# Attention on one Trainium2 core: the product with the values in 64x32 tiles of the array, fed by an exchange of weight quarters

## The chip, the cores and the metric

The kernel runs on one core of a Trainium2 chip. A core has five engines with instruction lists of their own: TensorE (PE in the profile; its weight loads are listed apart as PEld), VectorE (DVE), ScalarE (ACT), GpSimd (POOL) and SyncE (SP), which here only issues transfers (DMA). The engines wait for each other by semaphores; each works through its list in order. The metric is the device time of one execution in microseconds; runs are compared by their median.

## The reference

Cross attention of 16 batches with 1024 queries of 512 features and 64 context rows, 16 heads of 32, all in float32.

```python
xq  = (1 + scale_q)  * layernorm(x)       + shift_q     # scale, shift: silu(cond) @ Wss + bss
xkv = (1 + scale_kv) * layernorm(context) + shift_kv
q = (xq @ Wq + bq).reshape(B, Lq, 16, 32)
k, v = split(xkv @ Wkv + bkv)
scores = einsum('bqhd,bkhd->bhqk', q, k) / sqrt(32)
attn = softmax(scores, axis=-1)
o = einsum('bhqk,bkhd->bqhd', attn, v).reshape(B, Lq, 512)
return x + (o @ Wp + bp)
```

## The kernel before

**Blocks.** The 16 x 1024 query rows are cut into 32 blocks of 512 rows (NB = 32, two to a batch, BPB = 2). The context of eight batches at a time forms a group, "A" and "B". All lists are written out by hand: the order of the calls in the program is the order on each engine (`tc.manual_schedule()`).

**Way in.** Up to block 2 the calls stand one by one: the context's keys and values, the first blocks' features and queries, and the first score products. Then follows the loop over i = 3 to 29, and a way out written by hand.

**One turn of the loop.** It works on several blocks at once: scores of block i, value product and projection of a = i - 1, the rest of the projection of b = i - 2, queries of n = i + 1, features of f = i + 2, normalising and turning of i + 3. The query product and the projection are each done as seven products of half size with sums made beforehand (`seven` at line 547, `product` at line 958). Their sums are made on GpSimd (`feature_sums`, line 506; `row_sums`, lines 928 to 938).

**Scores.** `score_products` (line 666) makes for each half z of the 64 keys 16 matmuls, 32 rows (features of a head) by 32 columns (keys) by 512 queries. The result lies with partition 32 c + key for the four head groups c, and the four heads r of a group side by side. `maximum` and `maxima` (lines 683, 703, 712) find the maximum of each row and spread it into the tile mb, whose buffer has the tag "spread" and exists once; `subtract` (line 725, GpSimd) and `weights` (line 731, ScalarE's exponential) follow. So the weights of a block are two tiles, `s_tiles[i, 0]` and `s_tiles[i, 1]`, one for each half of the keys.

**Sums of the weights.** `total` (line 765, GpSimd) adds the two tiles, `row_total` (line 770) sums over the keys, `inverse_rows` takes the reciprocal (line 785), writes it to memory (`ltd`, line 788) and reads it back in another order by four transfers (`vr`, line 790). `spread_rows` (line 796) spreads it into vb, and `divided` (lines 809 and 814) multiplies the value product with it on its way out of the accumulators.

**Value product.** `mix` (line 834) has 32 matmuls: for each half z, head group c and head r one with 32 rows (the keys of that half), 32 columns (features of the head) and 512 queries; the second half adds onto the first in the accumulator. `V_all` holds the values to match: partition 32 c + key of the half, and along the free dimension batch, z and features. `value_move` (line 639) brings them there from `stages` in transfers of 32 partitions.

**Features.** `turn` (line 375) transposes 32x32 squares of normalised x into `ht` (one buffer); `move` (line 397) exchanges the squares between partition groups by 16 transfers of 64 KB into `xt` (two buffers); `scale_features` (line 455, ScalarE) applies scale and shift there.

**SyncE's list in the loop.** The two stores of block b (line 984), the residual's load (`load_residual`, line 127), the load of x (`load_x`, line 109), then `inverse_rows(i)`: the write ltd, a wait until it has landed, four reads vr; then the 16 transfers of `move(i + 3)`.

Of the kernel before, what the change touches and what calls it, by code (L numbers as in the profile page):

```python
# [20 lines left out]
def cross_attention_block(  # L21
# [369 lines left out]
    def move(i, two=False):  # L391

        ht = ht_tiles.pop(i)
        xt = features_tile(i)
        for k in range(4):
            for g in range(4):
                (nc.gpsimd if two and g % 2 else nc.sync).dma_start(  # L397
                    xt[32 * k : 32 * k + 32, g],
                    ht[32 * g : 32 * g + 32, k].rearrange("p c t b -> p c (t b)"),
                )  # L400
# [233 lines left out]
    def value_move(i, m):  # L634
        for c in (2 * m, 2 * m + 1):
            for j in range(2):
                for z in range(2):
                    at = j * LKV + z * HK
                    nc.sync.dma_start(
                        V_all[i][32 * c : 32 * c + 32, j::2, z, :],  # L640
                        stages[i][at : at + HK, :, c * P : (c + 1) * P],
                    )
# [115 lines left out]

    sum_tiles, lt_tiles, vt_rows = {}, {}, {}
# [22 lines left out]
    def inverse_rows(i):  # L782
# [3 lines left out]
        v = small.tile([P, NC, NJ], F32, tag="vr", name=f"vr_{i}")  # L786
        d = dram.tile([NC, 32, HPC, NJ], F32, tag="lt", name=f"ltd_{i}")
        nc.sync.dma_start(d.rearrange("c a r j -> (c a) r j"), lt)
        for r in range(HPC):
# [28 lines left out]
    def mix(i, apart=True, ks=(None,) * NC):  # L818
# [273 lines left out]
    turned_products()  # L1092
    turned_scaled(3)
    load_x(1)
    q_stats("B", (1,))
    load_x(2)
    turned_scaled(2)
    context_out("A", "v", 7)
    context_product("A", "k", 5)
    column_sums("q", w_q_sb, w_q_sums, (0,))  # L1100
    column_sums("q", w_q_sb, w_q_sums, (1,))
    context_out("A", "v", 5)
    load_projection()
    q_stats("B", (3,))
    turned_scaled(0)
    context_product("A", "k", 4)
    context_out("A", "k", 4)
    q_scale("B")
    context_out("A", "k", 5)
    q_stats(1, (0,))  # L1110
    turned_scaled(1)
    hidden("B", (3,))
    context_product("A", "v", 3)
    hidden("B", (2,))
    context_product("A", "k", 3)
    hidden("B", (1,))
    turned_features("B", 1)
    turned_features("B", 3)
    q_stats(1, (1,))
    hidden("B", (0,))  # L1120
    feature_sums(0, nc.gpsimd, (0,))
    turned_features("B", 0)
    feature_sums(0, nc.gpsimd, (1,))
    turned_features("B", 2)
    column_sums("q", w_q_sb, w_q_sums, (2,))
    context_out("A", "k", 3)
    q_stats(1, (3,))
    query_product(0, 1)
    feature_sums(0, nc.gpsimd, (2,))
    modulated("B", 0, 0, nc.scalar)  # L1130
    q_stats(1, (2,))
    q_scale(1)
    query_seed(0)
    modulated("B", 1, 0, nc.vector)
    context_product("A", "v", 4)
    context_out("A", "v", 3)
    hidden(1, (0,))
    modulated("B", 0, 0, nc.vector)
    hidden(1, (1,))
    turn(1, (0,))  # L1140
    load_x(3)
    hidden(1, (2,))
    load_projection_bias()
    query_product(0, 2)
    turn(1, (1,))
    turn(1, (2,))
    hidden(1, (3,))
    column_sums("q", w_q_sb, w_q_sums, (3,))
    turn(1, (3,))
    q_stats(2, (0,))  # L1150
    feature_sums(0, nc.gpsimd, (3,))
    q_stats(2, (3,))
    context_out("A", "v", 4)
    move(1, two=True)
    query_out(0, 2)
    query_product(0, 6)
    query_out(0, 6)
    modulated("B", 0, 1, nc.scalar)
    modulated("B", 1, 1, nc.vector)
    modulated("B", 0, 1, nc.vector)  # L1160
    modulated("B", 1, 1, nc.scalar)
    context_product("B", "k", 1)
    query_product(0, 5)
    feature_sums("B", nc.gpsimd, (0,))
    context_out("B", "k", 1)
    query_product(0, 7)
    q_stats(2, (1,))
    modulated("B", 1, 0, nc.scalar)
# [271 lines left out]
    for i in range(3, NB - 2):  # L1440
# [68 lines left out]
        if i + 3 < NB:  # L1509
            move(i + 3)  # L1510
# [138 lines left out]
```

## Time and profile before

| what | us |
|---|---|
| median of 3 runs (lowest to highest) | 1020.19 (1019.91 to 1021.4) |
| the profiled execution, its own time | 1021.49 |
| its span | 1019.7 |
| TensorE busy in the span | 1007.1 |
| VectorE / GpSimd / ScalarE busy | 864.3 / 808.1 / 637.6 |
| value product of one block, 64 records | 2.28 |
| score product of one half, 32 records | 1.07 |
| granted TensorE clock, mean of the span | 0.999 |

Columns of a row of groups are: line, engine, operation, output <- inputs, sizes, count. In a row of the stretches stand the stretch, its length and, engine by engine, busy time with the number of records that touch it, at the end the granted clock, the transfer engines' busy share and GB/s. A record that reaches over an edge is counted in both stretches. A matmul of float32 has two weight loads and two matmul records. In the time-ordered views the first two columns are start and length in us. SPq is SyncE's sequencer: an issue's length is the time that the list is occupied, not the transfer's.

### The profile page before, as it was taken

To read this page: it belongs to the slowest core of one execution; us is meant where nothing else is said; L and a number is where in the kernel's file an instruction comes from. 1 tells how busy PE (TensorE), PEld (TensorE's weight loads), DVE (VectorE), ACT (ScalarE), POOL (GpSimd) and SP (SyncE) were. 2 spreads that over 40 slices of the span, in tenths; PEclk is the share of its full clock that TensorE was granted. 3 is DMA by queue.
4 is the path that set the end of the run, shared out by engine and by line. 5 is a ranking of instruction groups with operands and counts; after the bars stand their busy time and mean duration, and the time that the engine had idled before them with its cause. 6 is when DMAs were issued, how large, how long until landed. Compare 5 with 4: busy or idle time off the path is not lost.

```text
span 1019.7 us, 21289 instructions
## 1 busy us (share of the span) xinstructions
PE 1007.1 (99%) x8109; PEld 770.6 (76%) x8109; DVE 864.3 (85%) x1184; ACT 637.6 (63%) x1025; POOL 808.1 (79%) x518
## 2 busy tenths in 40 slices
PE   8999999999999999999999999999999999999997
PEld 7887777777777777777777777877777778777746
DVE  6787889898889888988898888889888888876785
ACT  3688666666667666666666666666666666565520
POOL 2659898888898888888987887898888888987781
PEclk9999999999999999999999999999999999999999
DMA  9574544444445544444454453444543444345122
GB/s 301 199 217 131 150 173 146 126 133 150 156 156 165 167 128 127 134 153 153 151 168 131 127 165 123 152 160 157 167 142 116 124 158 153 112 126 168 44 77 95
DMA packets 112117, 149.82 MB, mean 147 GB/s; under 512 B 34024, under 2 KB 45312, under 8 KB 112016
## 3 DMA queue, kind: packets, MB, share of 16 engines
q1 hardware_dynamic: 111760, 147.95, 45.6%
q8 instruction: 64, 1.05, 0.4%
q0 software_dynamic: 256, 0.52, 0.2%
q14 instruction: 37, 0.30, 0.1%
HBM read 79.21 MB, written 34.60 MB: 112 GB/s over the span
## 4 chain that ended last, share of the span: by engine, by line
PE 88%; DVE 3%; POOL 3%; DMA 2%; ACT 1%; SPq 1%; issue 1%; DVEq 0%; POOLq 0%; ACTq 0%
PE pp L958 35%; PE pq L547 35%; PE po L834 7%; PE ps L666 6%; POOL s L725 2%; PE pp L861 1%; PE pk_A L547 1%; PE pv_A L547 1%; PE pk_B L547 1%; SPq L397 1%; ACT s L731 1%; DVE m L683 1%; DMA wss_kv<-in_L_xcond_Wss_kv_dram 1%; DMA x<-in_x_dram 1%; DVE mb L712 0%
## 5 line engine op out<-in xcount | busy, mean ns | idle before, releaser
L725 POOL TENSOR_TENSOR s<-s,mb 128x2048 f32<-128x2048 f32 x64 | 290.3, 4561 | 128.1 <-DVE mb L712 128.1
L692 ACT COPY s<-ps 128x1024 f32<-128x1024 f32 x128 | 129.4, 1012 | 102.6 <-DVE m L683 59.4
L683 DVE TRANSPOSE_TENSOR_REDUCE m<-ps 128x32 f32<-128x1024 f32 x128 | 151.4, 1217 | 33.2 <-PE ps L666 33.1
L958 PE MATMUL pp<-w_p_sb,ot 128*128 128x256 f32 x736 | 169.4, 380 | 1.3 <-DVE ot L814 0.9
L982 DVE TENSOR_TENSOR r<-pp,r 128x512 f32<-128x512 f32 x210 | 136.6, 671 | 30.0 <-PE pp L958 24.9
L958 PEld LDWEIGHTS pp<-w_p_sb,ot 128*128 128x128 f32 x736 | 139.9, 190 | 21.8 <-issue 1.8
L586 ACT ACTIVATE qt<-pq,bias_t 128x256 f32<-128x256 f32 x256 | 105.6, 463 | 74.0 <-PE pq L547 74.0
L731 ACT ACTIVATE s<-s 128x2048 f32<-128x2048 f32 x64 | 122.4, 1912 | 46.3 <-POOL s L725 46.2
L765 POOL TENSOR_TENSOR sum<-s,s 128x2048 f32<-128x2048 f32 x31 | 140.7, 4540 | 4.4 <-ACT s L731 4.4
L958 PEld LDWEIGHTS pp<-WT,s 128*128 128x128 f32 x496 | 89.8, 190 | 56.7 <-issue 28.5
L547 PE MATMUL pq<-xt_sums,w_q_sums 128*128 128x256 f32 x512 | 123.6, 385 | 0.0
L958 PE MATMUL pp<-WT,s 128*128 128x256 f32 x496 | 123.0, 391 | 0.0
L547 PE MATMUL pq<-xt,w_q_sb 128*128 128x256 f32 x512 | 121.4, 380 | 0.0
L547 PEld LDWEIGHTS pq<-xt_sums,w_q_sums 128*128 128x128 f32 x512 | 95.3, 190 | 34.2 <-issue 22.6
L547 PE MATMUL pq<-xt,w_q_sums 128*128 128x256 f32 x512 | 121.1, 380 | 0.0
L958 PE MATMUL pp<-WT,ot 128*128 128x256 f32 x496 | 117.3, 380 | 0.0
L547 PEld LDWEIGHTS pq<-xt,w_q_sb 128*128 128x128 f32 x512 | 97.1, 190 | 16.1 <-issue 3.4
L547 PEld LDWEIGHTS pq<-xt,w_q_sums 128*128 128x128 f32 x512 | 97.4, 190 | 13.3 <-ACT qt L586 0.3
L958 PEld LDWEIGHTS pp<-WT,ot 128*128 128x128 f32 x496 | 94.3, 190 | 13.4 <-POOL WT L896 0.8
L344 ACT ACTIVATE x<-x,rstdq 128x512 f32<-128x512 f32 x128 | 97.0, 808 | 2.0 <-POOL rstdq L319 2.0
L455 ACT ACTIVATE xt<-xt,ss_q 128x512 f32<-128x512 f32 x124 | 94.3, 808 | 5.5 <-DMA xt<-ht 3.8
L301 DVE BATCH_NORM_STATS2 bs<-x 128x6 f32<-128x512 f32 x128 | 87.0, 680 | 0.3 <-DMA x<-in_x_dram 0.3
(176 smaller groups left out, 1488.8 us busy)
## 6 DMA issues: line engine op xcount, KB each, us to landing
x<-in_x_dram SPq DMA_DIRECT2D x32, 1024.0 KB, 5.4
r<-in_x_dram SPq DMA_DIRECT2D x32, 1024.0 KB, 5.1
xt<-ht SPq DMA_DIRECT2D x488, 64.0 KB, 2.0
out_dram<-r SPq DMA_DIRECT2D x60, 512.0 KB, 3.7
wss_q<-in_L_xcond_Wss_q_dram SPq DMA_DIRECT2D x4, 512.0 KB, 10.1
vr<-ltd SPq DMA_DIRECT2D x128, 8.0 KB, 1.6
out_dram<-r SPq DMA_DIRECT2D x7, 256.0 KB, 2.2
x_A<-in_ctx_dram SPq DMA_DIRECT2D x4, 256.0 KB, 3.0
```

The source lines that it names most:

```text
L301: nc.vector.bn_stats(bs, r)
L344: nc.scalar.activation(dst, src, AF.Identity, bias=rstd[:, 1, j : j + 1], scale=rstd[:, 0, j : j + 1])
L455: nc.scalar.activation(xt[:, :, c, :], xt[:, :, c, :], AF.Identity, scale=ss["q"][:, c, b : b + 1], bias=ss["q"][:, NC + c, b : b + 1],)
L547: nc.tensor.matmul(out_, lhsT=lhsT, rhs=rhs, start=new and m == 0 and c == 0, stop=c == HC - 1, skip_group_check=True,)
L586: nc.scalar.activation(dst, src, AF.Identity, bias=bq_t[:, o : o + 1])
L683: nc.vector.tensor_reduce(m_tiles[i][:, z, 2 * e : 2 * e + 2, :], s_banks[i, z][e].rearrange("p r (j a) -> p r j a", a=32), AX.X, ALU.max, ...
L692: nc.scalar.copy(s_tiles[i, z][:, 2 * e : 2 * e + 2, :], s_banks[i, z][e])
L725: eng.tensor_tensor(s_tiles[i, z], s_tiles[i, z], mb_tiles[i], ALU.subtract)
L731: nc.scalar.activation(p, p, AF.Exp, scale=SCALE)
L765: nc.gpsimd.tensor_tensor(t, s_tiles[i, 0], s_tiles[i, 1], ALU.add)
L958: nc.tensor.matmul(acc[k][:, t * HO : (t + 1) * HO], lhsT=rows[:, c, t * P : (t + 1) * P], rhs=cols[:, c, :], start=n == 2 and t == 0 and ...
L982: nc.vector.tensor_add(r, a, r)
```

## The change

**Value product in 64x32 tiles.** For blocks 2 to 29 (`paired`) a matmul takes all 64 keys of a head at once: 16 matmuls of 64 rows by 32 columns by 512 queries, without adding up in the accumulator. The head groups go in the order 0, 2, 1, 3, so that rows 0 to 63 and rows 64 to 127 take turns. Blocks 0, 1, 30 and 31 keep the 32 matmuls.

**Exchange.** For that the two weight tiles of a block are rearranged: in each half of the partitions the upper quarter of the first tile and the lower quarter of the second change places, by way of a third tile `t` with the tag "spread" (mb's buffer). Three steps, each two transfers of 32 partitions x 4 x 512 floats.

**Values.** `value_move` takes one head group c a call and lays the values in the new order, but for the batch of blocks 0 and 1 and that of blocks 30 and 31, which keep the old one; their part goes by transfers of its own, 6 a call instead of 4.

**Order.** `inverse_rows` is split into `inverse_out` (reciprocal and write) and the reads; in the loop the swaps and parts of `move` are set between them. `load_residual(i)` stands ahead of `biased(a, 2)`. The way in, from `turned_products()` to the loop, is in a new order.

```diff
+    def paired(i):
+        return BPB <= i < NB - BPB
+    def swap(i, step):
+        if not paired(i):
+            return
+        first, second = s_tiles[i, 0], s_tiles[i, 1]
+        if step == 0:
+            swaps[i] = rpool.tile([P, HPC, TB], F32, tag="spread", name=f"swap_{i}")
+        t = swaps[i]
+        for at in (0, 64):
+            low, high = slice(at, at + 32), slice(at + 32, at + 64)
+            if step == 0:
+                nc.sync.dma_start(t[high], second[low])
+            elif step == 1:
+                nc.sync.dma_start(second[low], first[high])
+            else:
+                nc.sync.dma_start(first[high], t[high])
...
     def mix(i, apart=True, ks=(None,) * NC):
...
+        if paired(i):
+            for c in (0, 2, 1, 3):
+                rows = slice(64 * (c // 2), 64 * (c // 2) + 64)
+                for r in range(HPC):
+                    nc.tensor.matmul(
+                        po[c][32 * r : 32 * r + 32, :],
+                        lhsT=vt[rows, c % 2, 32 * r : 32 * r + 32],
+                        rhs=s_tiles[i, c % 2][rows, r, :],
+                        start=True,
+                        stop=True,
+                    )
+            return
...
-    def value_move(i, m):
+    def value_move(i, c):
+        for j in range(2):
+            for z in range(2):
+                at = j * LKV + z * HK
+                src = stages[i][at : at + HK, :, c * P : (c + 1) * P]
+                p = 64 * (c // 2) + 32 * z
+                dst = V_all[i][p : p + 32, j::2, c % 2, :]
+                plain = {("A", 0): 0, ("B", 1): NT - 1}.get((i, j))
+                if plain is None:
+                    nc.sync.dma_start(dst, src)
+                    continue
+                rest = slice(1, NT) if plain == 0 else slice(0, NT - 1)
+                nc.sync.dma_start(dst[:, rest], src[:, rest])
+                nc.sync.dma_start(
+                    V_all[i][32 * c : 32 * c + 32, 2 * plain + j, z, :], src[:, plain]
+                )
```

In the way in, the place that the prediction speaks of (as it stands after; in the list before, `move(1, two=True)` came ahead of `query_out(0, 2)`, `value_move("A", 0)` after it, and `scale_features(1, (1,))`, the first of them, after `query_out(0, 3)`):

```python
    query_product(0, 4)
...
    value_move("A", 0)
    move(1, two=True)
...
    context_product("B", "k", 2)
...
    scale_features(1, (0,))
    turn(2, (0,))
    query_product(0, 3)
    query_added(0, 4)
...
    query_out(0, 3)
...
    score_products(0, 0)
```

In the loop:

```diff
         added(b, 4)
         added(b, 3)
+        load_residual(i)
         biased(a, 2)
-        load_residual(i)
         mix(a)
...
         row_sums(a, 1)
+        swap(i, 0)
         if i < NB - 3:
             turn(i + 3, range(NT))
         if i < NB - 5:
             load_x(i + 5)
...
         query_product(n, 3)
         query_out(n, 3)
+        swap(i, 1)
         feature_sums(f)
         product(a, 7)
+        if i + 3 < NB:
+            move(i + 3, (0,))
         row_total(i)
+        inverse_out(i)
+        swap(i, 2)
+        if i + 3 < NB:
+            move(i + 3, (1,))
         inverse_rows(i)
         if i + 3 < NB:
-            move(i + 3)
+            move(i + 3, (2, 3))
```

More of the change, by code (lines that the diff above doesn't have):

```diff
@@ L1426, in cross_attention_block @@
+    subtract(2, zs=(1,))
+    biased(1, 2)
+    divided(1)
+    turn(5, (2,))
+    query_out(3, 7)
+    turn(5, (3,))
+    weights(2, 0)
+    scale_features(4, (1,))
+    weights(2, 1)
+    row_sums(1, 0)
+    load_residual(2)
+    swap(2, 0)
+    query_product(3, 5)
+    query_added(3, 5)
+    q_stats(6, (1,))
+    load_x(7)
+    product(1, 1)
+    total(2)
+    scale_features(4, (2,))
+    swap(2, 1)
+    added(1, 1)
+    query_product(3, 4)
+    product(1, 2)
+    q_stats(6, (3,))
     added(1, 2)
```

551 lines of the change are left out of this document (269 added, 282 removed).

## The prediction

> **What bounds the kernel now.** First the page's busy times and its chain of waits:
>
> ```profile
> span 1019.7 us, 21289 instructions
> PE 1007.1 (99%) x8109; PEld 770.6 (76%) x8109; DVE 864.3 (85%) x1184; ACT 637.6 (63%) x1025; POOL 808.1 (79%) x518
> PE 88%; DVE 3%; POOL 3%; DMA 2%; ACT 1%; SPq 1%; issue 1%; DVEq 0%; POOLq 0%; ACTq 0%
> PE pp L958 35%; PE pq L547 35%; PE po L834 7%; PE ps L666 6%; POOL s L725 2%; PE pp L861 1%; PE pk_A L547 1%; PE pv_A L547 1%; PE pk_B L547 1%; SPq L397 1%; ACT s L731 1%; DVE m L683 1%; DMA wss_kv<-in_L_xcond_Wss_kv_dram 1%; DMA x<-in_x_dram 1%; DVE mb L712 0%
> ```
>
> TensorE is the bound; what another engine saves is worth nothing unless TensorE waits for it. Where does it wait? The busy times of stretches (columns: stretch, length, then busy time and count of each engine):
>
> ```profile
> 40.00:70.00 30.00, 30.00 (x174) 25.58 (x174) 23.17 (x56) 27.05 (x66) 19.00 (x30) 1.00 0.64 201
> 70.00:104.00 34.00, 33.27 (x236) 25.62 (x243) 25.94 (x36) 27.35 (x46) 25.91 (x20) 1.00 0.50 141
> 166.00:966.00 800.00, 798.59 (x6553) 611.81 (x6552) 693.96 (x905) 516.11 (x800) 664.78 (x399) 1.00 0.45 142
> ```
>
> In 800 us of the loop it is free for 1.4, and between 40 and 104, in the way in that is reordered, for 0.73. So an edit pays only by taking work off TensorE, and costs only where its inputs come late. One turn of the loop in the chain, in order of time (start, length):
>
> ```profile
> 503.72 1.07 PE ps L666 x32
> ...
> 516.62 2.28 PE po L834 x62
> ...
> 533.00 1.07 PE ps L666 x32
> ```
>
> A turn is 533.00 - 503.72 = 29.28 us, of which the product with the values (po) is 2.28 and each score product (ps) 1.07.
>
> **The product itself.** [...] A score product is 16 matmuls on the 16 tiles of 32x32, two steps; the value product is 32 on the same 16 tiles, four steps. How these steps lie, by counts of records that touch a stretch (PE, then weight loads):
>
> ```profile
> 516.50:517.00 0.50, 0.45 (x16) 0.23 (x32) 0.00 (x0) 1.00 0.45 111
> 517.00:517.43 0.43, 0.43 (x32) 0.10 (x1) 0.00 (x0) 1.00 0.23 62
> 517.43:517.60 0.17, 0.17 (x17) 0.10 (x1) 0.00 (x0) 1.00 1.04 252
> 517.60:518.05 0.45, 0.45 (x31) 0.37 (x30) 0.00 (x0) 1.00 0.20 50
> ```
>
> Sixteen tiles stream together; the next sixteen follow at 517.00, 0.45 later; at 517.43 one tile has its successor, after a stream of 0.43, but the other fifteen, and their 30 weight loads, come only from 517.60 on. That hold of about 0.19 falls where the second half of the keys (z = 1) begins.
>
> Afterwards a matmul takes 64 rows and 32 columns, so 16 matmuls on 8 tiles: two on each, two passes each, again four steps. The number of instructions halves; the streaming doesn't. No row shows 64x32 tiles. From above: hold and spread as now, 2.28. From below, by instructions alone, half of 2.28, 1.14; excluded, since each tile must stream four times 0.43 = 1.72. Nearest is a product that also reuses tiles and also is only 16 matmuls, in the preamble, on 128x32 tiles, four tiles with eight steps:
>
> ```profile
> 28.52 1.08 PE L263 MATMUL ss_q<-wss_q,early 128*32 128x128 f32 x32
> 28.75:28.86 0.11, 0.11 (x12) 0.11 (x8) 0.00 (x0) 0.00 (x0) 1.00 1.07 382
> 28.86:28.97 0.11, 0.11 (x12) 0.11 (x8) 0.00 (x0) 0.00 (x0) 1.00 1.01 363
> ```
>
> Every step of 0.11 (a quarter of 0.43, with a quarter of the columns) has the same counts: no hold when a tile takes its next weights. So I take the score product, 16 matmuls without hold at 1.07, and add two steps of 0.43, less 0.05 as eight tiles start in half the spread of sixteen (about 0.1): 1.07 + 0.86 - 0.05 = **1.88**, 0.40 less than 2.28. Blocks 2 to 29: 28 x 0.40 = **11.2 us**.
>
> **What must be there in time.** Per block six transfers of 32 partitions x 8 KB (256 KB) join SyncE's list; their forms are not in the trace. Nearest rows: issues and landings by size, SyncE's queue, and who waits there:
>
> ```profile
> xt<-ht SPq DMA_DIRECT2D x488, 64.0 KB, 2.0
> vr<-ltd SPq DMA_DIRECT2D x128, 8.0 KB, 1.6
> x_A<-in_ctx_dram SPq DMA_DIRECT2D x4, 256.0 KB, 3.0
> L639 SPq DMA_DIRECT2D V_A<-stage_A x16: 587/602/668, 61.8 to 87.2; - x16
> 47.63 1.15 SPq L200 DMA_DIRECT2D w_p_sb<-in_L_xcond_Wp_dram  x1
> 505.15 0.34 SPq L788 DMA_DIRECT2D ltd<-lt  x1
> 508.48 1.75 SPq L790 DMA_DIRECT2D vr<-ltd  x4
> 510.32 11.35 SPq L397 DMA_DIRECT2D xt<-ht  x16
> ```
>
> An issue costs between 0.34 and 1.15 us; I take 0.60, the row that also is 32 partitions wide. Landing 3.0. The readers, on the other engines:
>
> ```profile
> 497.66 4.53 POOL L765 TENSOR_TENSOR sum<-s,s 128x2048 f32<-128x2048 f32 x1
> 504.57 0.55 DVE L785 RECIPROCAL lt<-lt 128x64 f32<-128x64 f32 x1
> 512.75 2.31 DVE L712 STREAM_TRANSPOSE mb<-m 128x2048 f32<-128x2048 f32 x1
> 514.99 2.27 DVE L796 STREAM_TRANSPOSE vb<-vr 128x2048 f32<-128x2048 f32 x1
> 517.18 1.25 DVE L982 TENSOR_TENSOR r<-pp,r 128x512 f32<-128x512 f32 x2
> 518.86 2.36 DVE L814 TENSOR_TENSOR ot<-po,vb 128x1024 f32<-128x1024 f32 x2 [0.43 <-issue]
> 520.66 3.62 PE L958 MATMUL pp<-w_p_sb,ot 128*128 128x256 f32 x16
> 523.39 1.52 ACT L455 ACTIVATE xt<-xt,ss_q 128x512 f32<-128x512 f32 x2 [0.94 <-DMA xt<-ht]
> 524.82 1.89 ACT L731 ACTIVATE s<-s 128x2048 f32<-128x2048 f32 x1
> ```
>
> Swap step 0 waits for the second exponential, which ends 526.71; two issues; x's load behind them leaves at most 1.2 later, and its tile is first read a turn on. Step 1 waits for the sum, 497.66 + 4.53 = 502.2 (a turn earlier by the clock, same place): to 503.4. Four moves at 11.35/16 = 0.71: to 506.2, where now the list stands idle for lt, ready at 505.1. inverse_out to 506.6 (now 505.5). Step 2 to 507.8, landed 510.8 at the latest. Four moves to 510.6; meanwhile ltd has landed (now 508.48 - 505.15 = 3.3 after its issue, so 509.5). The four vr to 512.4, landed 514.0. The eight moves left to 518.1 instead of 521.7.
>
> So: the spread tile, which step 0 takes from mb, is free at 510.8; mb needs it at 512.75: 1.9 spare. The product with the values comes at 516.6: 5.8 spare. vr is needed at 514.99: 1.0 spare. The moved features come 3.6 us earlier, and ACT's 0.94 of waiting goes; behind it stands slack, worth 0. Behind vr on VectorE stand two additions and the division, and behind the division TensorE's next projection. In the shorter turn that product is asked for at 520.26; the division's first half ends at 518.46 + 1.2 = 519.7. I cost the swaps at **0**.
>
> The value moves grow from 16 to 24 per group (the two blocks of a batch end that stay plain), in the way in only, 8 x 0.60 us of SyncE's time each. The load of the residual moved ahead of biased changes no queue: the one is SyncE's, the other ScalarE's. The swaps' bytes, 28 x 1.5 MB, lift the transfer engines' share in the loop from 0.45 (the column before the last in the long stretch) to about 0.6 if they run like the rest; that is cover enough.
>
> **The way in.** TensorE does the same matmuls; the 0.73 that it is free there is about all there is to win back, and one place looks tight: value_move("A", 0), six transfers, now stands ahead of move(1), and scale_features(1, (0,)) ahead of query_out(0, 3), which the first scores need.
>
> ```profile
> 54.86 0.66 DVE L632 TENSOR_TENSOR stage_A<-pv_A,stage_A 128x512 f32<-128x512 f32 x1
> 64.44 0.84 ACT L586 ACTIVATE qt<-pq,bias_t 128x256 f32<-128x256 f32 x2
> 67.78 1.14 PE L666 MATMUL ps<-qt,K_A 32*32 32x512 f32 x32
> ```
>
> If the stage is complete where it is now, at 55.5: six issues at 0.60 to 59.1; SyncE's eight moves at 0.71 to 64.8; landed 66.8; scaled (0.76) 67.6; query_out 68.4; the scores wait 0.6 past 67.78. With 1.15 an issue it is 3.9. Bounds: -1 (the 0.73 goes, nothing new) to +4. I take **+1**, nearer to 0.6, with something for places of this kind that I can't see.
>
> **Sum.** The profiled execution took 1021.5 us, span 1019.7 and 1.8 around it: 1021.5 - 11.2 + 0 + 1 = 1011.3. The median of the runs is 1.3 below that execution, so **1010**; own range 1005 to 1014 (way-in bounds, and 1.88 by 0.1 either way at 28 blocks, not both at their ends).
>
> **Rivals.** *The hold stays.* The loads for c = 1 wait until the matmuls of c = 0 in the same rows are through. These take 0.588:
>
> ```profile
> L834 PE MATMUL po<-s,V_A x1024: 585/588/613, 103.9 to 547.6; 32*32 32x512 f32 x171
> ```
>
> Third step at 0.45 + 0.59 + 0.03 = 1.07 instead of 0.88, the product 2.07; 28 x 0.21 = 5.9 saved, 1015. For it: the hold seen now. Against: the preamble's product, whose loads run while other tiles of the same rows stream. [...]
>
> *The change doesn't do what it says*: the two row halves don't stream together. Eight steps instead of four, 1.88 + 4 x 0.43 = 3.6, 28 x 1.32 = 37 lost: 1059. [...]
>
> *SyncE's list is too long* (the other side): steps 1 and 2 cost 1.15 an issue, not 0.60. vr lands 4 x 0.55 = 2.2 later, at 516.2, 1.2 past its reader; the division's first half ends 517.18 + 1.2 + 1.25 + 0.43 + 1.2 = 521.3, and TensorE waits 1.0 at 520.26. That takes back the 0.40 and 0.6 more: 28 x 0.6 = 17 lost, with the way in 1021.5 + 17 + 1 - 1.3 = 1038. It decides from vr 1.6 later than in my sum, where TensorE's wait reaches the 0.40 and the time is near 1021. For it: spare of only 1.0. Against: the row of the same width.
>
> **Numbers.** Forecast 0.60, hold stays 0.18, list too long 0.14, halves apart 0.08. About 0.2% (2 us) is what a measurement of this kernel tells from no change. Faster: nearly all of the first two, less a way in that eats them, 0.71; within 0.2%: 0.07, from the list near its turning point and the hold with a bad way in; slower: 0.22, the list, the halves, and the rest of the way in. The range runs from 1003, the own range with the uncertainty of the unseen tiles, to 1030, which takes in about half of the list's case; outside lie the halves and the list at full price.
>
> **What would show it.** In the profile after: 32 records of po per block, 1.9 us from its first to the next product, four even steps; turns of 28.9 us; the six swaps near 0.6 an issue; mb and vb without waits on transfers; and po in line with TensorE near 99%. Wrong if po keeps 2.3, if VectorE's L796 or L712 waits on DMA in every turn, or if TensorE stands idle over 2 us between 40 and 110.

## The result and the profile after

The changed kernel takes **1060.65 us** (median of 4 runs, 1057.96 to 1061.92) against 1020.1 us of the kernel before beside it (4 runs): 1.0391 times as long, 95% interval 1.0369 to 1.0413. The forecast was 1010, with the other sign. The profiled execution took 1060.88, its span is 1059.1.

The page of the changed kernel, chain of waits by engine and by line:

```profile
PE 31%; DMA 22%; POOL 15%; DVE 11%; SPq 10%; issue 7%; ACT 3%; DVEq 0%; POOLq 0%; ACTq 0%
PE pp L1009 13%; PE pq L548 12%; DMA s<-s 10%; POOL s L733 10%; SPq L398 6%; DMA swap<-s 5%; POOL sum L795 4%; DMA s<-swap 3%; DVE mb L720 3%; DVE vb L835 2%; PE ps L674 2%; DMA vr<-ltd 2%; ACT s L739 2%; DVE ot L853 2%; SPq L829 1%
```

TensorE made 88% of this chain before; now transfers, GpSimd, VectorE and SyncE's list carry 58% of it, and the exchange's three forms (s<-s, swap<-s, s<-swap) stand among its largest lines.

Where the time went, stage by stage, follows from two rows of each kernel: the first and the last product with the values in the new form (blocks 2 and 29). First before, then after, both from the view in order of time:

```profile
165.99 2.35 PE L834 MATMUL po<-s,V_A 32*32 32x512 f32 x64
...
966.21 2.55 PE L834 MATMUL po<-s,V_B 32*32 32x512 f32 x64
```

```profile
170.69 1.95 PE L872 MATMUL po<-s,V_A 64*32 64x512 f32 x32
...
1005.06 2.00 PE L872 MATMUL po<-s,V_B 64*32 64x512 f32 x32
```

| us | before | after |
|---|---|---|
| way in, to block 2's product | 166.0 | 170.7 |
| loop, from there to block 29's product | 800.2 | 834.4 |
| rest of the span | 53.5 | 54.0 |

So 4.7 of the 39.4 us of span were lost in the way in, 34.2 in the loop and 0.5 behind it. The busy times of the same kernel (after), by stretches:

```profile
70.00:104.00 34.00, 31.49 (x219) 23.57 (x218) 25.83 (x39) 23.48 (x43) 25.05 (x20) 1.00 0.61 163
104.00:170.00 66.00, 63.71 (x505) 48.77 (x504) 54.05 (x70) 42.77 (x68) 54.53 (x35) 1.00 0.56 160
170.00:950.00 780.00, 748.68 (x5285) 564.43 (x5284) 659.62 (x864) 489.44 (x763) 623.57 (x380) 0.99 0.69 191
```

TensorE now stands idle for 31.3 of these 780 us of the loop, and for 4.8 in the 100 us ahead of it. Who waits for whom (line that waited, what ended the wait, us in total, times, longest):

```profile
PE pp L1009 <- DVE ot L853: 31.3, 21, 2.7
DVE mb L720 <- DMA s<-swap: 23.0, 16, 2.7
DVE vb L835 <- DMA vr<-ltd: 19.8, 22, 3.8
SPq L785 <- DMA swap<-s: 88.7, 43, 5.6
```

TensorE's projection waits for the division (ot); VectorE, which makes it, was held at the two places that the prediction named, mb and vb, by transfers; and SyncE's list itself stands still until one step of the exchange has landed and the next may go. The landings (KB of each transfer, median us from issue to landing):

```profile
x<-in_x_dram SPq DMA_DIRECT2D x32, 1024.0 KB, 8.9
swap<-s SPq DMA_DIRECT2D x56, 256.0 KB, 4.9
s<-s SPq DMA_DIRECT2D x56, 256.0 KB, 5.8
s<-swap SPq DMA_DIRECT2D x56, 256.0 KB, 3.9
```

One turn that stalls, SyncE's list in order of time (start, length):

```profile
303.53 0.38 SPq L127 DMA_DIRECT2D r<-in_x_dram  x1
305.61 1.15 SPq L783 DMA_DIRECT2D swap<-s  x2
306.96 0.70 SPq L109 DMA_DIRECT2D x<-in_x_dram  x1
310.77 2.30 SPq L785 DMA_DIRECT2D s<-s  x2
313.12 2.75 SPq L398 DMA_DIRECT2D xt<-ht  x4
315.91 0.58 SPq L819 DMA_DIRECT2D ltd<-lt  x1
318.33 1.14 SPq L787 DMA_DIRECT2D s<-swap  x2
319.52 3.91 SPq L398 DMA_DIRECT2D xt<-ht  x4
323.53 1.98 SPq L829 DMA_DIRECT2D vr<-ltd  x4
```

The other engines in the same turn:

```profile
306.20 4.54 POOL L795 TENSOR_TENSOR sum<-s,s 128x2048 f32<-128x2048 f32 x1
...
323.51 2.31 DVE L720 STREAM_TRANSPOSE mb<-m 128x2048 f32<-128x2048 f32 x1 [2.07 <-DMA s<-swap]
326.79 2.31 DVE L835 STREAM_TRANSPOSE vb<-vr 128x2048 f32<-128x2048 f32 x1 [0.96 <-DMA vr<-ltd]
330.20 2.34 DVE L853 TENSOR_TENSOR ot<-po,vb 128x1024 f32<-128x1024 f32 x2
331.55 5.38 PE L1009 MATMUL pp<-w_p_sb,ot 128*128 128x256 f32 x16 [2.41 <-DVE ot L853]
```

The sum is ready at 310.74. The prediction gave the way from there to the landing of step 2 at 8.6 us (502.2 to 510.8) and to that of vr 11.8 (to 514.0). Here step 2 lands 12.8 after the sum (mb starts at 323.51) and vr 16.0 after it (326.79). The spares were 1.9 and 1.0; the overrun is 4.2 at both. VectorE is late twice, and TensorE waits 2.4 us.

### The profile page after: what moved, and what is told of

Same layout as the page of the kernel before. It is cut to its first block, busy times and chain, and to the rows that moved or that the text cites. A ratio compares the mean times of both kernels' runs of the same rounds, so it can differ in the third digit from the quotient of the medians.

```text
span 1059.1 us, 19882 instructions
## 1 busy us (share of the span) xinstructions
PE 1011.7 (96%) x7213; PEld 763.8 (72%) x7213; DVE 864.5 (82%) x1184; ACT 637.4 (60%) x1025; POOL 808.2 (76%) x518
## 4 chain that ended last, share of the span: by engine, by line
PE 31%; DMA 22%; POOL 15%; DVE 11%; SPq 10%; issue 7%; ACT 3%; DVEq 0%; POOLq 0%; ACTq 0%
PE pp L1009 13%; PE pq L548 12%; DMA s<-s 10%; POOL s L733 10%; SPq L398 6%; DMA swap<-s 5%; POOL sum L795 4%; DMA s<-swap 3%; DVE mb L720 3%; DVE vb L835 2%; PE ps L674 2%; DMA vr<-ltd 2%; ACT s L739 2%; DVE ot L853 2%; SPq L829 1%
## 5 line engine op out<-in xcount | busy, mean ns | idle before, releaser
L1009 PE MATMUL pp<-w_p_sb,ot 128*128 128x256 f32 x736 | 181.4, 398 | 31.8 <-DVE ot L853 31.3
L1009 PEld LDWEIGHTS pp<-w_p_sb,ot 128*128 128x128 f32 x736 | 144.7, 200 | 62.6 <-ACT pp L967 37.0
L739 ACT ACTIVATE s<-s 128x2048 f32<-128x2048 f32 x64 | 122.3, 1911 | 28.9 <-POOL s L733 28.3
L720 DVE STREAM_TRANSPOSE mb<-m 128x2048 f32<-128x2048 f32 x32 | 74.0, 2312 | 28.0 <-DMA s<-swap 23.0
```

What stands on the lines that cost most here:

```text
L720: nc.vector.transpose(t, src.unsqueeze(2).to_broadcast([P, HPC * NJ, 32]))
L739: nc.scalar.activation(p, p, AF.Exp, scale=SCALE)
L1009: nc.tensor.matmul(acc[k][:, t * HO : (t + 1) * HO], lhsT=rows[:, c, t * P : (t + 1) * P], rhs=cols[:, c, :], start=n == 2 and t == 0 and ...
```

## The experiments

The edits are against the changed kernel unless another is named. Times are medians of several runs, ratios against the kernel before on the same chip; "one run" is a single execution.

**The product and the exchange apart.** First the exchange left out, the new product kept (it then meets weights in the wrong place, so that only the time is of use):

```diff
     def swap(i, step):
-        if not paired(i):
-            return
+        return
```

> The changed kernel without the exchange (the weight tiles stay as they are, so the product takes wrong rows); everything else as after, the 64x32 product, the new way in and the split moves among it. Theory 'late exchange': TensorE's 36 us of waiting between 60 and 1000 and its six stretches at half clock all come from the exchange's three chained transfers, so the loop runs at 28.8 us a turn with TensorE idle under 2 us in it; 1020 - 11.2 + about 4 for the way in's new waits = 1013 us. Rival 'new order': the split of move and inverse_rows and the way in cost of themselves; then the time stays above 1025 us. Rival 'product': the 64x32 tiles slow their neighbours on TensorE; then it stays above 1020 with TensorE busy throughout.

Measured: 1012.25, ratio 0.9931 (0.9914 to 0.9948). Its loop in the same two views:

```profile
169.27 1.95 PE L871 MATMUL po<-s,V_A 64*32 64x512 f32 x32
...
956.45 2.00 PE L871 MATMUL po<-s,V_B 64*32 64x512 f32 x32
```

```profile
170.00:950.00 780.00, 780.00 (x5624) 594.18 (x5609) 688.46 (x900) 511.58 (x797) 659.45 (x399) 1.00 0.47 145
```

The loop is 787.2 us, 13.0 shorter than before, without a gap on TensorE, and a turn in it is 28.80. The product's gain is real, and the exchange costs 834.4 - 787.2 = 47 us in the loop. Then the other half alone, the exchange with the old 32 matmuls (here too only the time is of use):

```diff
-        if paired(i):
+        if False:
             for c in (0, 2, 1, 3):
```

> The changed kernel with the old 32 matmuls of 32x32 in every block (the values lie in the new order, so they meet the wrong weights); the exchange stays. Theory 'late exchange', as a circle: mb of a block, subtraction, exponential, sum, exchange step 1, step 2, and mb of the next block in the same buffer form a circle of about 31 us that doesn't go through TensorE; so it sets the turn whatever the product takes, and the time is that of after within 4 us, 1058 to 1064 us. Rival 'additive': TensorE's waits stay and the 11.2 us of the product come back on top: 1072 us.

Measured: 1063.18, ratio 1.0429 (1.0413 to 1.0446). With 11 us more of TensorE's work it takes only 2.5 us more than the changed kernel, so TensorE's work no longer sets a turn's length. One rival has to be looked at: in the profiled execution TensorE's projection waits as long for the division as in the changed kernel (30.4 us against 31.3), but the granted clock is 0.997 on the mean and not 0.990, which by my estimate (0.007 of a span of 1063.1) is 7 us and would make up for most of the 11. The four executions speak against it: with mean clocks of 0.997, 0.995, 0.994 and 0.993 they took 1064.93, 1063.31, 1063.06 and 1062.51, so the one with the lowest clock was the shortest. Then the same six transfers with a quarter of the bytes, one head of four:

```diff
-                nc.sync.dma_start(t[high], second[low])
+                nc.sync.dma_start(t[high, :1], second[low, :1])
```

and so for the other two steps.

> The changed kernel with the same twelve... six transfers per block, in the same places and with the same waits, but each with one head of four (64 KB instead of 256 KB; the other heads stay unexchanged). Theory 'late exchange' with the landing times set by bytes in the queues: landings fall from 4 to 6 us to about 2.5, mb waits no longer, about 1015 us. Rival 'fixed cost': the three round trips and SyncE's waits for them are what is late, whatever their size: above 1040 us.

One run: 1014.85, close to the time without any exchange. Its landings:

```profile
swap<-s SPq DMA_DIRECT2D x56, 64.0 KB, 3.1
s<-s SPq DMA_DIRECT2D x56, 64.0 KB, 2.0
s<-swap SPq DMA_DIRECT2D x56, 64.0 KB, 2.0
```

Same issues, same waits, same order. So neither the number of issues nor the waits as such cost 47 us: it is how long 256 KB take to land, three times in a row.

**The buffer of the third tile.** If mb waits for step 2 because they share a buffer, give the third tile another, that of vb:

```diff
-            swaps[i] = rpool.tile([P, HPC, TB], F32, tag="spread", name=f"swap_{i}")
+            swaps[i] = qpool.tile([P, HPC, TB], F32, tag="vb", name=f"swap_{i}", bufs=1)
```

> The changed kernel with the exchange's third tile in vb's buffer (idle from the division to the next spread of vb) instead of mb's. Same bytes, same order of the transfers. Theory 'late exchange' by mb's buffer: mb never waits for a transfer any more and the circle is cut; vr still comes late, behind step 2 in SyncE's list, so a part of the waits stays: 1025 to 1045 us, VectorE's vb waiting for vr or for the exchange. Rival 'bytes': what costs is the traffic and the late list, not the buffer: 1055 us and more.

Measured: 1061.19, ratio 1.0425 (1.0368 to 1.0482), a miss: it lies in the range of the rival, by which the buffer is not what costs. Its waits:

```profile
DVE vb L835 <- DMA vr<-ltd: 52.3, 25, 3.9
PE pp L1009 <- DVE ot L853: 35.9, 21, 3.3
```

The wait at mb is gone, all of it moved to vb, from 19.8 to 52.3 us: vr stands behind the exchange in SyncE's list, and the time is as before. So mb's buffer is not needed for the loss; the wait at vb alone is enough.

**What makes the landings long.** Two runs. The 1 MB load of x moved from in front of step 1 to behind step 2:

```diff
-        if i < NB - 5:
-            load_x(i + 5)
...
         swap(i, 2)
+        if i < NB - 5:
+            load_x(i + 5)
```

> After, with the 1 MB load of x(i+5) moved in SyncE's list from between the first and second step of the exchange to behind the third. If the second step's landing of 5.8 us comes from the load in front of it in the queues, its landing falls to 3 to 4 us, the chain is 2 to 3 us shorter and the loop loses its 1.7 us per turn: 1015 to 1035 us. If the load then only delays the reading back of the divisor behind it (vr spare is under 1 us): 1055 to 1085 us, with ltd or vr landing 2 to 4 us later than now (3.4 and 1.7 us).

One run: 1120.27, above both of the ranges given. Step 1 does land in 3.3 instead of 5.8, as expected of the load in front of it. But the load now sits in front of vr:

```profile
DVE vb L835 <- DMA vr<-ltd: 85.4, 28, 5.2
```

And each transfer cut in two by heads, so that its rows are pieces of 2 KB:

```diff
-                nc.sync.dma_start(t[high], second[low])
+            for o in range(2):
+                nc.sync.dma_start(t[high, o::2], second[low, o::2])
```

and so for the other two steps.

> After, with each transfer of the exchange cut in two by heads (every second head), so that its rows are 2 KB pieces and not 8 KB: twelve issues per turn instead of six, the same bytes. If the 8 KB packets (about 550 ns each in the records, 2 KB ones of the loads 84 ns) make the landing slow, four pieces take 4 x 84 = 336 ns, a step takes 1.3 us of the 16 engines instead of 2.2, and the landings fall by about 1 us each: three steps, 3 us per turn less on the late chain, against about 1.1 us more of issue for each of three steps, so a gain of 0 to 3 us at the vr rows: 1040 to 1060 us with median landings of 3 to 4 us. If the rate between partitions is the same for either size, landings stay at 4 to 6 us and the doubled issue makes it worse: 1065 to 1100 us.

One run: 1102.61, just above the second range; the landings are 4.6, 5.8 and 2.5, so all but the last as long as with 8 KB, and twelve issues a turn make the list longer. The size of the pieces is not the cause.

**An earlier exchange.** Turned round, so that step 0 reads only the first weight tile and needs only the first exponential; vb's buffer; reading back of the divisor ahead of twelve moves and not eight:

```diff
-                nc.sync.dma_start(t[high], second[low])
+                nc.sync.dma_start(t[low], first[high])
...
-                nc.sync.dma_start(second[low], first[high])
+                nc.sync.dma_start(first[high], second[low])
...
-                nc.sync.dma_start(first[high], t[high])
+                nc.sync.dma_start(second[low], t[low])
...
-        load_residual(i)
         biased(a, 2)
...
         weights(i, 0)
+        swap(i, 0)
+        load_residual(i)
...
         row_sums(a, 1)
-        swap(i, 0)
...
         swap(i, 2)
-        if i + 3 < NB:
-            move(i + 3, (1,))
         inverse_rows(i)
         if i + 3 < NB:
-            move(i + 3, (2, 3))
+            move(i + 3, (1, 2, 3))
```

> The same three transfers per half block, turned round so that the first one needs only the first half of the weights: it copies first[high] into the third tile as soon as the first exponential is done, before the residual load, instead of after the second exponential and behind it; the third tile lies in the buffer of the spread divisor, so the maxima's tile waits for no transfer; and the last rows of turned features go behind the reading back of the divisor. Nothing else changes; bytes, number of transfers and TensorE's work stay. Theory of the late chain (the turn is set by second exponential, sum, three transfers in a row, reading back of the divisor): the chain from the second exponential holds two transfers instead of three, one landing of 4.9 us and one issue of 1.15 us shorter, against a loss of 1.7 us per turn now, so the loop is mostly without stalls: 1012 to 1022 us, TensorE idle between 166 and 1000 us under 8 us, no more than two stretches of half clock. Rival, bytes (the 1.5 MB of exchange per turn in SyncE's queue make every transfer slow, the divisor's included, wherever they are set): 1040 to 1060 us.

Measured: 1022.1 (10 runs, 1019.0 to 1027.8), ratio 1.0025 (1.0007 to 1.0042): 38 us back. SyncE's list in a turn of it:

```profile
299.62 0.39 SPq L109 DMA_DIRECT2D x<-in_x_dram  x1
304.01 1.15 SPq L785 DMA_DIRECT2D s<-s  x2
305.21 2.85 SPq L398 DMA_DIRECT2D xt<-ht  x4
308.16 0.53 SPq L819 DMA_DIRECT2D ltd<-lt  x1
311.32 1.15 SPq L787 DMA_DIRECT2D s<-swap  x2
312.82 2.70 SPq L829 DMA_DIRECT2D vr<-ltd  x4
```

Step 1 issues its two transfers in 1.15, not 2.30, since step 0 has long landed; vr begins 8.8 after it and not 12.8, as one landing and no second set of moves stands between. The landings are little shorter (4.6, 4.9, 3.8; x 8.4): the bytes are the same, and of the 48 us that the exchange cost 10 are left once two landings, not three, lie behind the second exponential and vr no longer stands behind the second set of moves.

The same without its last part, against the early exchange:

```diff
         swap(i, 2)
+        if i + 3 < NB:
+            move(i + 3, (1,))
         inverse_rows(i)
         if i + 3 < NB:
-            move(i + 3, (1, 2, 3))
+            move(i + 3, (2, 3))
```

> The early exchange without its last part: turned round, third tile in the divisor's buffer, first step behind the first exponential, but four moves of the turned features still ahead of the reading back of the divisor, as in the kernel after. It tells the parts of the early exchange apart: the buffer alone gave nothing (1061). If the early first step is what frees the chain: 1022 to 1030 us, the divisor's rows some 2 us later than with all three parts. If the order at the end of the turn did it: 1040 to 1060 us.

Measured: 1031.07, ratio 1.0109 (1.0095 to 1.0123), 1 us above the first range. So the buffer alone brought nothing, the early step with it 30 us, the four moves 9 more.

In seven of its turns the early exchange still takes 29.1 to 30.7 us. Two tries to mend that; neither did. Both edits are against the early exchange. First two sets of moves ahead of the reading back, one of them ahead of step 1:

```diff
+        if i + 3 < NB:
+            move(i + 3, (0,))
         swap(i, 1)
+        if i + 3 < NB:
+            move(i + 3, (1,))
...
         product(a, 7)
-        if i + 3 < NB:
-            move(i + 3, (0,))
...
         inverse_rows(i)
         if i + 3 < NB:
-            move(i + 3, (1, 2, 3))
+            move(i + 3, (2, 3))
```

> The early exchange, with the first sixteen-row set of the turned features' moves issued ahead of the second step (whose wait for the sum otherwise holds them in SyncE's list for about 3 us) and the second set right behind that step. In the early exchange eight turns of 27 took 29.1 to 30.7 us and not 28.8, some 5.8 us in all, and a stalled turn has ScalarE waiting 1.3 us for the features' landing. If the wait of the second step is what makes the features late, those turns go to 28.8: 1015 to 1019 us, and it beats the kernel before by 1 to 5 us. If instead the second step, held behind four more issues, becomes late and with it the reading back of the divisor: 1020 to 1028 us.

Measured: 1026.58, ratio 1.0065 (1.0052 to 1.0079), in the second range: step 1 and the reading back come later, and VectorE waits 23.0 us for vr instead of 6.0. Then step 0 issued by ScalarE:

```diff
-                nc.sync.dma_start(t[low], first[high])
+                nc.scalar.dma_start(t[low], first[high])
```

> The early exchange with its first step (two transfers per block, both ready when ScalarE's own first exponential is) issued by ScalarE and not by SyncE. Against the run without any exchange the early exchange takes 9.8 us more, 5.8 of it in the loop, in turns of 29.1 to 30.7 us. If SyncE's list (the two issues, its wait for the first exponential, and the r and x loads and the features' moves behind it) makes those turns long: turns of 28.8, 1015 to 1019 us, faster than the kernel before. If ScalarE, which then issues 1.2 us more per turn between its first exponential and the query's output, becomes late: TensorE waits on ScalarE's qt in most turns, 1024 to 1035 us.

Measured: 1047.06, ratio 1.0272 (1.0254 to 1.0289), above both ranges. ScalarE's list in one turn, and the waiting in the whole run:

```profile
359.01 1.16 ACTq L783 DMA_DIRECT2D swap<-s  x2
```

```profile
PE pq L548 <- ACT qt L587: 18.1, 26, 1.3
```

ScalarE has no 1.2 us to spare at that point: the query's output behind the issue comes late and TensorE waits in 26 turns, which become 29.6 us. Why the early exchange is still some 10 us above the run without any is not settled by this. In its profiled execution (1020.16) the loop takes 5.8 us more than without the exchange, 3.8 of them idle time of TensorE; moving issues to either of the two other places only made it longer.

**The way in.** The early exchange with the order of before in the way in (the value moves cut as in the changed kernel, the exchange of block 2 put in), here against the list of before:

```diff
     weights(2, 1)
+    swap(2, 0)
...
+    swap(2, 1)
+    move(5, (0,))
     row_total(2)
...
+    inverse_out(2)
+    swap(2, 2)
     inverse_rows(2)
     q_scale(6)
-    move(5)
+    move(5, (1, 2, 3))
```

> The early exchange of the run before, with the order of the way in as it was before the change (only the value moves split by block column and the exchange of block 2 put in). TensorE's idle time between 40 and 170 us was 0.7 us in the kernel before and 4.8 in the kernel after: if the new order alone made that, this is 3 to 5 us faster than the early exchange with the new order. With a stall-free loop it then beats the kernel before by its product's 11 us less what the exchange still costs: 1007 to 1017 us. If instead the two sets of pieces of the value moves (more, smaller transfers) made the idle time, the two versions have the same time within 2 us.

Measured: 1025.36, ratio 1.0053 (1.0032 to 1.0074), a miss: block 2's product starts at 176.6 there, 5 us later than with the new order. So the order is not what costs. Then the kernel before with nothing but the value moves cut finer, every piece to its old place:

```diff
-                    nc.sync.dma_start(
-                        V_all[i][32 * c : 32 * c + 32, j::2, z, :],
-                        stages[i][at : at + HK, :, c * P : (c + 1) * P],
-                    )
+                    src = stages[i][at : at + HK, :, c * P : (c + 1) * P]
+                    dst = V_all[i][32 * c : 32 * c + 32, j::2, z, :]
+                    plain = {("A", 0): 0, ("B", 1): NT - 1}.get((i, j))
+                    if plain is None:
+                        nc.sync.dma_start(dst, src)
+                        continue
+                    rest = slice(1, NT) if plain == 0 else slice(0, NT - 1)
+                    nc.sync.dma_start(dst[:, rest], src[:, rest])
+                    nc.sync.dma_start(dst[:, plain], src[:, plain])
```

> The kernel before, with nothing of the change but the count of the value moves: 24 transfers per context half and not 16, every piece still going to its old place, the order of the way in left alone. Theory A (the finer value moves are what makes the way in late; the stage buffer is held longer and VectorE and GpSimd wait for it): block 2's product starts 3 to 8 us later than the 166.0 us of the kernel before, and the whole takes 1022 to 1029 us. Theory B (the new order of the way in is what costs, whatever the pieces): start at 166 and 1019 to 1021 us.

Measured: 1031.04, ratio 1.0107 (1.0078 to 1.0135), the first of the two theories, and 2 us above its range. Sixteen transfers more, once per kernel, cost 11 us. The second group's moves in the kernel before, and GpSimd's first use of WT, whose buffer holds the staged values until they have left:

```profile
108.93 10.37 SPq L639 DMA_DIRECT2D V_B<-stage_B  x16
...
121.50 1.28 POOL L892 TENSOR_TENSOR WT<-w_p_sb 128x512 f32<-128x512 f32 x1
```

The same with finer moves:

```profile
111.09 1.32 SPq L643 DMA_DIRECT2D V_B<-stage_B  x2
...
127.76 0.59 SPq L647 DMA_DIRECT2D V_B<-stage_B  x1
129.74 1.26 POOL L897 TENSOR_TENSOR WT<-w_p_sb 128x512 f32<-128x512 f32 x1 [5.80 <-DMA V_B<-stage_B]
```

In the kernel before the last value leaves at 119.3, while GpSimd is still busy with a sum to 121.5, so nobody waits. With 24 issues it leaves at 128.4, GpSimd waits 5.8, TensorE 5.0 for WT, and block 2's product starts at 176.4 and not 166.0. The granted clock of this execution is 0.997 on the mean of its span of 1028.8 us, against 0.999 before; what part of the 10.4 us that makes is not shown here. Is it SyncE's list or the landing? The sixteen small pieces on ScalarE's queue, in the kernel before:

```diff
-                    nc.sync.dma_start(dst[:, plain], src[:, plain])
+                    nc.scalar.dma_start(dst[:, plain], src[:, plain])
```

> The kernel before with the finer value moves of e9_before_pieces, the sixteen small pieces (16 KB each) issued from ScalarE's queue and not SyncE's. The finer moves cost 11.2 us there, with 5.0 us of TensorE idle before the products that need WT, whose buffer the staged values still hold. If SyncE's list is what is long (16 more issues of about 0.6 us, 4.8 us for each context half, in front of what follows), most of the cost goes: 1020 to 1024 us. If the transfers themselves (their landing of 2 to 4 us, the last of the set late) hold the buffer, it stays: 1028 to 1033 us.

Measured: 1026.84, ratio 1.0067 (1.0045 to 1.0089): between the two. SyncE's issues end 6 us earlier (122.4), but WT still comes at 129.6, and TensorE waits 4.1 for it; the trace puts the end of GpSimd's wait on a landing of the features' moves (xt<-ht), no longer on the values. The same pieces on ScalarE's queue in the early exchange, with the new order:

```diff
-                nc.sync.dma_start(
+                nc.scalar.dma_start(
                     V_all[i][32 * c : 32 * c + 32, 2 * plain + j, z, :], src[:, plain]
                 )
```

> The early exchange, with the sixteen small pieces of the value moves issued from ScalarE's queue. Way in now: block 2's product starts at 171.4 us against 166.0 in the kernel before, TensorE idle 3.9 us between 40 and 170. If SyncE's issues make that, the start falls to 167 to 170 and the whole to 1017 to 1020 us, faster than the kernel before by up to 3 us. If ScalarE becomes late by its 16 issues (9 us in all), or the landings hold the buffer: 1022 to 1028 us.

Measured: 1025.82, ratio 1.0058 (1.0036 to 1.008). And the same edit with the old order:

> The early exchange with the old order of the way in (e8_old_way, block 2's product at 176.6 us, 4.7 us of TensorE idle before WT), with the small pieces on ScalarE's queue. If the issues in SyncE's list are the cause, the 4.7 us of idle and the half clock behind it go, the start falls to 167 to 170 us and the whole to 1014 to 1019 us: a version faster than both. If not, it stays at 1023 to 1028 us.

Measured: 1023.46 (10 runs, 1018.19 to 1028.74), ratio 1.0031 (1.0008 to 1.0054). None of them beats the kernel before; the early exchange comes nearest. What holds WT once SyncE's list is shorter stays open.

## Why the prediction was wrong

**The product: right, to the hundredth.** 28 x 0.40 us was forecast from 1.88 for the new product. The 32 records of po in a block reach to the next product in 1.88 us in 27 blocks (2.47 in the last, in the way out, where it was 2.66 before), and in all 28 in four steps at 0, 0.45, 0.88 and 1.31; the run without the exchange gains 13.0 in the loop (the rest of it are two turns near 30 us in the loop before), and its turns are 28.8, forecast 28.9. So the rival "the hold stays", 2.07 for the product, is refuted here: the loads for the second matmul of a tile did run while the other column groups of the same rows streamed (in the product that begins at 358.39, the sixteen loads of the second matmuls lie in two rows of eight from 358.84 and from 359.27 on, each beside eight streaming tiles). "Halves apart" gives nearly the measured time, 1059, and is refuted by the same 1.88; the figure is a coincidence.

**"I cost the swaps at 0": the step that failed.** Its issue price was right (1.15 for two measured, 0.60 for one taken). The **landing of 3.0 us** was wrong: it came from 256 KB loads of the preamble, and in place of it the exchange measured 4.9, 5.8 and 3.9, with 1 MB loads in front of two of its steps. Step 1 cannot go before step 0 has landed, nor step 2 before step 1, nor mb before step 2, so the error came three times. In the turn shown, the second transfer of step 1 has to wait for step 0 and leaves 1.1 later than forecast; the list then stands idle for 1.8, from 316.49 to 318.33, until step 1 has landed, where the forecast had no wait; and step 2 takes 1.0 longer to land. That is the 4.2 us at mb, where 1.9 were to spare. vr does not wait for step 2's landing; there the third part is the four moves in front of it, 3.91 us in place of 2.84, and 4.2 late with 1.0 to spare. A quarter of the bytes (1014.85) undoes nearly all of the loss; the early exchange (1022.1) four fifths, 30 us by the early step and 9 by the moves. The prediction's own statement "cover enough" for the bytes counted the transfer engines' mean share, 0.6 forecast and 0.69 measured; a mean says nothing of a chain of three transfers.

**Lateness was costed once, not round the circle.** The readers were set against a clock that TensorE keeps. But a late step 2 makes mb late, mb the subtraction, the exponential and the sum, and these the next exchange: lateness that is handed on from turn to turn. The turns are 28.8 to 33.4 us long, where TensorE's work alone takes 28.8, and the exchange with 11 us more matmul takes 2.5 us more, as such a loop of its own would have it. By which way it closes is argued here, not shown: mb's buffer is not needed for it, as the run with vb's buffer shows (no wait at mb, the same time); the other way goes from vr by vb and VectorE's list, and no run cut that one alone.

**The rival on that side** (SyncE's list too long, 1038) had place and sign right, vr, VectorE's division, TensorE's wait, but put it on an issue of 1.15 us, which was 0.58 (1.15 for two); it decided "from vr 1.6 later", and vr came 4.2 later.

**The way in, +1, bounds -1 to +4**: 4.7 measured; without the exchange it is 3.3 (169.27 against 165.99). The place named, the scores at 67.8, was not late. What TensorE waited for instead (the longest wait of each row, 1.6, 1.5 and 0.7, lies in the way in):

```profile
PE ps L674 <- ACT s L700: 2.1, 2, 1.6
PE pp L1009 <- POOL WT L947: 1.5, 1, 1.5
PE pp L1009 <- POOL WT L945: 0.7, 1, 0.7
```

So 2.2 of its 4.8 us of idle time go to the term that was costed as "SyncE's time" alone: sixteen more issues delay the release of the staging buffer, and so WT (GpSimd waits 3.3 us for the last value to leave). With the old order they cost 10.4 at block 2's product; the new order takes back about half. Another 1.6 are one score product at 101.12 that waits for ScalarE's copy of earlier scores; the runs with the old order don't have this wait, and what makes the copy late stays open.

**Not in the sum at all: the clock.** From one product to the next it is 33.12 us in the turn with the wait shown above (2.41 us, up to 331.55), and 28.94 in the next, which has none. Stretches of the kernel after (before the last two columns, the granted clock):

```profile
325.27:358.39 33.12, 30.71 (x210) 23.09 (x209) 28.04 (x36) 19.22 (x30) 25.73 (x16) 0.95 0.66 185
358.39:387.33 28.94, 28.94 (x209) 21.90 (x208) 24.54 (x35) 19.18 (x30) 23.96 (x16) 1.00 0.70 196
331.50:335.00 3.50, 3.45 (x10) 2.87 (x11) 2.19 (x4) 3.37 (x5) 3.50 (x2) 0.62 0.80 300
```

The wait is 2.4 of the 4.2 us between them; the rest is the half clock behind it: the 16 projection records of 331.55 take 5.38 us, where the row before the change has 3.62. In the trace of the clock such a stretch at one half is 3.41 us long, and there are six of them in the loop: 6 x 3.41 / 2 = 10 us of the 47. TensorE's idle time in the loop is 31 more. The last 6 go with the waits as well: a turn with a wait and no half clock is 0.2 us longer than 28.8 and its wait, as from 294.21 to 325.27, 31.06 us with a wait of 2.03. In a stream the matmul records of 0.38 us start every 0.22 and overlap (as at 365 us); across the wait ahead of 331.55 the next starts 2.41 after the last has ended.

These are shares of one sum, not three savings. The run with vb's buffer has a granted clock of 0.994 and 35.9 us of waits for the division in a span as long (1058.9 us), that with the old product 0.997 and 30.4 in 1063.1, the changed kernel 0.990 and 31.3 in 1059.1: the runs that lost less to the clock are shorter by 0.2 us at most.

## What to carry to other kernels

Before a transfer is set into a list at "no cost", follow the chain that it joins to its end, with the landing of a transfer of the same shape beside the same loads, and count how many such landings stand in a row: here three of 4.9, 5.8 and 3.9 us stood where 3.0 each had been set, and in the turn shown the end came 4.2 late. Ask also whether the late end feeds the next turn's start; here it did, and TensorE waited 21 times, 31.3 us in all. Where a buffer is released by the last of several transfers, ask who takes it next before cutting them finer: here 24 transfers in place of 16, without a byte more, held GpSimd up for 5.8 us and cost 11.

## What the hardware showed that I had not expected

**Half clock after short waits.** The six stretches at half clock in the changed kernel's loop begin at 209.47, 332.35, 424.51, 578.11, 759.02 and 881.90 us; each is 3.413 us long at a granted clock of 0.50, and the beginnings lie whole multiples of 3.413 us apart (36, 27, 45, 53 and 36 of them). Waits of TensorE of 2.4 to 2.7 us stand ahead of all six, while waits of 2.0 and 2.1 us in the same run, at 298.09 and 666.02, had none behind them. In the 3.41 us just ahead of each of the six TensorE is idle for 2.2 to 2.6; of the other stretches of this length in the loop, laid end to end from the same beginnings, none has more than 1.90. So in this run each wait that left TensorE idle for over 2.2 us of such a stretch cost 1.7 us of its time (half of 3.413) beyond itself. What sets the beginnings, and whether the same holds at other lengths of wait, is not shown by this run.

**Copies between partitions.** A packet of 8 KB from one quarter of the partitions to another takes 0.56 us at the median of the changed kernel's 5376 (15 GB/s), one of 2 KB of a load 0.084 (24 GB/s), and with rows cut to 2 KB the first two steps took about as long to land (4.6 and 5.8 us, against 4.9 and 5.8). The features' moves in the kernel before, 2 KB packets between all sixteen pairs of quarters (the same quarter, and 32, 64 and 96 partitions apart), take 0.145 us at the median (14 GB/s), and in two sets with no load beside them, issued from 450.0 and 479.3 us on, 0.142 to 0.147 in each of the sixteen. So the lower rate doesn't depend on how far apart the quarters are; where it comes from stays open.

**ScalarE's queue is no free list.** Two issues there took 1.16 us of ScalarE's own time, as on SyncE (1.15), and cost 25 us in all (1047.06 against 1022.1).
